# Where row weights, stores, exponentials and the last output groups stand in a convolution-attention-MoE kernel

## The chip, the cores and the metric

The kernel runs on one core of one Trainium2 chip. A core has a matrix engine (TensorE, called PE in the profile), three engines for elementwise work (VectorE or DVE, ScalarE or ACT, GpSimd or POOL), a synchronisation engine (SyncE or SP) that issues most transfers, and 16 DMA engines. The metric is the device time of one execution in microseconds (us); lower is better. "Before" is the median of 3 runs, 1987.64 us (1986.89 to 1988.37). One further execution was profiled.

## What is computed

The input x has two images of 256 channels and 56 x 56 pixels, in float32. Two layers follow.

Layer 0 works on each image: group norm, a 1x1 convolution to 768 channels (q, k and v), a depthwise 3x3 convolution of these, and 7 x 7 neighbourhood attention with 8 heads of 32 channels. The first four heads use dilation 1, the other four dilation 2. A projection is added to x.

```python
x = x + _L0_conv_ref(_gn(x), w_qkv1, w_qkv2, rpb0, rpb1, w_proj)
t = _to_tokens(x)                          # 2 * 3136 = 6272 tokens of 256
t = t + _L1_attn_ref(_ln_t(t), ...)        # linear attention and a feed-forward net
t = t + _L1_ffn_ref(_ln_t(t), ...)         # 8 experts, the best 2 for each token
```

Layer 1 works on the tokens. `_L1_attn_ref` is linear attention (elu + 1 on queries and keys) with a merge, two layer norms and a feed-forward net of width 512. `_L1_ffn_ref` routes each token to the two experts with the largest logits. The two weights follow from the difference of the two logits by one exponential. Each expert is a gelu net of 256 to 1024 to 256. The weighted sum of both experts is added to the token.

## The kernel before

All matmuls are in float32. The work is arranged so that PE always has something to do, and its own order is written out by hand (`tc.manual_schedule`). The order on the other engines comes from a scheduler at build time, which takes priorities, readiness and the ties `tc.issue_after(x)` ("not ahead of x") into account. What one engine does is therefore a fixed queue, and an instruction whose operand is late holds up all that stand behind it on that engine. The stages, in us from the span's start:

- 0 to 440: convolutions, and attention of image 1.
- 440 to 745: convolutions of image 2 together with the linear layer on the first half of the tokens (`linear(ph, tk, 0)`). Letters in `parts` say the order: keys, queries, message, feed-forward, route, prob and so on.
- 735 to 1045: attention of image 2. The last groups' routing (`ending`) and the first expert tiles run beside it.
- 1045 to 1440: the linear layer on the second half, with expert tiles interleaved.
- 1440 to 1970: the remaining expert tiles, in 39 slots. 34 are full tiles of 256 rows and 5 are half tiles of 128.
- 1970 to 1991: reading, turning and storing the last groups of the output.

Tokens are handled in groups of 4 blocks of 128. `route` (L2028) finds the two experts of each token (`top_two`) and the place of its row in its experts' lists. The sums over tokens are the matmuls L2083 and L2084 with the result `slot` (L2086). `weights` (L2018) takes the exponential of the difference of the logits on ACT (L2021). After it `store` (L1981) puts the tokens themselves into the result array y2 from ACT's queue (L1985), and POOL scatters the normalised rows into the experts' lists xs (helper at L168). ACT also computes gelu (hT, L1611), and gelu and the exponential need different tables, which ACT_TABLE_LOAD changes.

An expert tile goes through three steps. `fetch` (L1534) reads the expert's number, issues the loads of its rows xr (L1543) and its weights (L1547, L1551), and computes the rows' weights `eq` and row numbers `idi` on DVE (L1557 to L1561). `turn` (L1570) transposes the rows on PE (px, L1576), applies the norm's scale (xe, L1579), loads the bias b2 (L1584) and starts the result yt with it (L1589). `run` (L1591) does the first matmuls (ph, L1607), gelu, the second matmuls (py, L1625), the weighted addition (L1631) and the scatter that adds the rows to y2. In a full tile ph and py are 32 matmuls each.

When attention of image 2 begins, `prepare` (L796) loads rows of queries and keys (ld, L803), which PE turns (x, L766), and `settle` (L771) copies them to qT0 (L775), kT0 (L778), qT1 (L784) and kT1 (L791). `fetch` of the attention loads tables for the position bias (tab, L713), bands load their values (v0, L862; v1, L982), and each block has scores (s_ps, L651), an exponential (L655), the product with the table (p, L656) and the product with the values (po, L665). At this change the space of the first half's token tiles goes over to the attention.

In the last stage `between` is called once for each slot. From slot `first` (29) on, in nine slots, it starts the `read` (L2340) of one output group from y2. One slot later `write` turns it on PE (pto, L2352), copies it (L2358) and stores it (L2364). Behind the slots, each engine reads the number of surplus tiles (`more`, L2389), which a branch would run; here there are none. Then the last five groups are read all together, turned and stored.

Of the kernel before, what the change touches and what calls it, by code (L numbers as in the profile page):

```python
# [64 lines left out]
FILLS = (0, 2, 12, 18, 24, 27, 33)  # L65
ENDING = (4, 6, 13, 15, 20)
XW = C + 4


def shape_constants():  # L70
# [56 lines left out]
def hybrid_kernel(ctx: ExitStack, tc: tile.TileContext, a: dict, out: bass.AP):  # L127
# [46 lines left out]

    evac_n = [0]

    newest = [None, None, None]

    def evac(dst, src):

# [425 lines left out]
    class Attention:  # L606
# [116 lines left out]
        def run(self):  # L723
# [47 lines left out]
            def settle(g, k, pm):  # L771

                r0 = 4 * g
                if k == 0:
                    nc.scalar.mul(qT0[:, 2 * r0 : 2 * r0 + 8, :].rearrange("p r c -> p (r c)"), pm[:, :G], SCALE)  # L775
# [578 lines left out]
    class Experts:  # L1354
# [179 lines left out]
        def fetch(self, t, nh, pools):  # L1534

            run = self.tk.run
            full = nh == 2 and t < NTA
            tab, k = (self.tab_h, t) if nh == 1 else (self.tab_a, t) if full else (self.tab_b, t - NTA)
            x = SimpleNamespace(t=t, nh=nh, full=full)
            xr = x.xr = pools.xr()[:, :nh, :]  # L1540
            e = self.value(tab.tab[0:1, 0, k : k + 1], E - 1)
            r = self.value(tab.tab[0:1, 1, k : k + 1], E * RG + (NDUM - 1) * ST)
            ins = nc.sync.dma_start(xr, xs[bass.ds(r, nh * P), :].rearrange("(p j) c -> p j c", j=nh))  # L1543
            if full:
                apart(ins.ins, [f"xfull{run}"], [f"xlate{run}", f"fill{run}"])
            x.w1 = self.w.tile([P, 2, FF], F32, name="w1e")
            nc.sync.dma_start(  # L1547
                x.w1, a["L1_ffn_W1"][bass.ds(e, 1)].rearrange("one (ct p) f -> p (one ct) f", p=P)
            )
            x.w2 = self.w.tile([P, NJ, C], F32, name="w2e")  # L1550
            nc.sync.dma_start(  # L1551
                x.w2, a["L1_ffn_W2"][bass.ds(e, 1)].rearrange("one (j p) d -> p (one j) d", p=P)
            )
            x.e = e
            x.eq = self.small.tile([P, 2], F32, name="eq")
            eq = x.eq[:, :nh]
            nc.vector.tensor_scalar(eq, xr[:, :, C + 3], tab.etm[:, k : k + 1], None, ALU.is_equal)  # L1557
            x.idi = self.small.tile([P, 2], mybir.dt.int32, name="idi", bufs=4)
            nc.vector.tensor_copy(x.idi[:, :nh], xr[:, :, C])  # L1559
            nc.vector.tensor_tensor(eq, eq, xr[:, :, C + 2], ALU.mult)  # L1560
            nc.vector.tensor_tensor(eq, eq, xr[:, :, C + 1], ALU.add)  # L1561
# [6 lines left out]
            return x  # L1568

        def turn(self, x, pools):  # L1570

            nh = x.nh
            px = pools.px()
            for ct in range(2):
                for j in range(nh):
                    nc.tensor.transpose(px[:, ct, j, :], x.xr[:, j, ct * P : (ct + 1) * P], ident)  # L1576
            x.xe = pools.xe()[:, :, : nh * P]
            for ct in range(2):
                newest[0] = nc.vector.tensor_scalar(  # L1579
                    x.xe[:, ct, :], px[:, ct, :nh, :].rearrange("p j t -> p (j t)"),  # L1580
                    x.sv[:, ct : ct + 1], x.sv[:, 2 + ct : 3 + ct], ALU.mult, ALU.add,
                ).ins
            b2 = pools.b2e()
            nc.sync.dma_start(  # L1584
                b2, a["L1_ffn_b2"][bass.ds(x.e, 1)].rearrange("one d -> (one d)").partition_broadcast(P)
            )
            x.yt = pools.yt()
            for h in range(nh):
                nc.gpsimd.tensor_scalar(x.yt[:, h, :], b2, x.eq[:, h : h + 1], 1.0, ALU.mult, ALU.mult)  # L1589

        def run(self, ts, pools, between=lambda i: None):  # L1591
# [7 lines left out]
            for i, (t, nh) in enumerate(ts):  # L1599
# [4 lines left out]
                for j in range(NJ):  # L1604
                    p1 = pools.ph()[:, : nh * P]
                    for ct in range(2):
                        nc.tensor.matmul(  # L1607
                            p1, x.w1[:, ct, j * P : (j + 1) * P], x.xe[:, ct, :],
                            start=(ct == 0), stop=(ct == 1),
                        )  # L1610
                    nc.scalar.activation(hT[:, j, :], p1, AF.Gelu, bias=x.sv[:, 4 + j : 5 + j])  # L1611
                    if j % 2:
                        yield
                between(i)
# [32 lines left out]
    def linear(ph, tk, half, behind=None):  # L1647
# [290 lines left out]
        def feed_forward(n0, n, m2T, out):  # L1938
# [3 lines left out]
            for oc in range(4):  # L1942
                p1 = ps_h.tile([P, 512], F32, name="p1", tag="h")
                for k in range(4):
# [1 line left out]
                    nc.tensor.matmul(  # L1946
                        p1[:, :w], fw1[:, k, oc * P : (oc + 1) * P], rhs, start=(k == 0), stop=(k == 3)
                    )
                nc.scalar.activation(hT[:, oc, :w], p1[:, :w], AF.Relu, bias=hb[:, oc : oc + 1])
                yield  # L1950
            ss = sm.tile([P, 4], F32, name="ssf")
            lb = routing[-1].sm.tile([P, 4, E], F32, name="lb")
# [28 lines left out]
        def store(n0, n):  # L1981

            for k0 in range(0, n, 2):
                kn = min(2, n - k0)
                ins = nc.scalar.dma_start(  # L1985
                    y2[(n0 + k0) * P : (n0 + k0 + kn) * P, :].rearrange("(n p) c -> p n c", p=P),
                    tk.at(n0 + k0, kn),
                )
# [29 lines left out]
        def weights(rt, ms, row, n):  # L2018

            r = rt.sm.tile([P, 4], F32, name="rsum")[:, :n]  # L2020
            nc.scalar.activation(ms[1], ms[1], AF.Exp)  # L2021
# [154 lines left out]
    def layer1(whole, tk, conv_ctx=None, conv=None, behind=None):  # L2176


        run = tk.run
        conv = conv or none  # L2180

        def fill(n=1):
            for _ in range(n):
# [64 lines left out]
        def experts():  # L2248
# [5 lines left out]
        xc = experts() if run else None  # L2254
        pools = SimpleNamespace(
            turn=lambda: tc.issue_after(newest[1]),
            xr=lambda: xc.tile([P, 2, XW], F32, name="xr"),
            xe=lambda: xc.tile([P, 2, ST], F32, name="xe"),
            yt=lambda: xc.tile([P, 2, C], F32, name="yt"),
# [24 lines left out]

        with ExitStack() as ph:
            ln = linear(ph, tk, 1)
            pools.px = lambda: ln.ps_a.tile([P, 2, 2, P], F32, name="px", tag="a")
            pools.ph = lambda: ln.ps_q.tile([P, 2, ST], F32, name="ph", tag="q")[:, 0, :]
            summed = []
# [25 lines left out]
        with ExitStack() as ph:  # L2315
# [8 lines left out]
            ps_t = ph.enter_context(tc.tile_pool(name="p4pt", bufs=2, space=PSUM, reuse_waits="tile"))  # L2324
            pools = SimpleNamespace(
                turn=nullcontext,
                xr=lambda: xp.tile([P, 2, XW], F32, name="xr"),
                xe=lambda: xp.tile([P, 2, ST], F32, name="xe"),
                yt=lambda: xp.tile([P, 2, C], F32, name="yt"),
# [17 lines left out]
            def write(n0, n, yr, engines, places):  # L2347
                for ct in range(2):
# [12 lines left out]
                    for b in range(B):  # L2361
                        c0, c1 = max(n0 * P, b * T), min((n0 + n) * P, (b + 1) * T)
                        if c0 < c1:
                            engines[ct].dma_start(  # L2364
                                ov[b, ct, :, c0 - b * T : c1 - b * T], o_sb[:, c0 - n0 * P : c1 - n0 * P]
                            )

# [6 lines left out]

            def between(i):

                if held:
                    write(*held.pop(0), (nc.scalar, nc.scalar), [(ps_t, "pt")] * 2)
                if first <= i < first + early2:
                    held.append(read(*order[i - first], True))  # L2380
# [8 lines left out]
            more = nc.values_load(  # L2389
                ex.more[0:1, 0:1], min_val=0, max_val=NTL,  # L2390
                skip_runtime_bounds_check_because="the number of tiles is bounded by the counts",
            )
            with tc.If(more > 0):
                for _ in ex.run([(t, 2) for t in range(NFS, NTL)] + [(k, 1) for k in range(NHS, E)], pools):
                    pass
            last = [read(n0, n, False) for n0, n in order[early2:]]
            for h in held + last:
                write(*h, (nc.scalar, nc.sync), [(ps_t, "pt"), (ps_h, "ph")])

    with ExitStack() as ph:  # L2400
# [3 lines left out]
        rest = first_image(conv, ph)  # L2404
        layer1(ph, tokens, conv_ctx, rest, anchors["residual4"])
    bad = nc.values_load(
        bad[0:1, 0:1], min_val=0, max_val=1, skip_runtime_bounds_check_because="a comparison's result"
    )
    with tc.If(bad > 0):
        with ExitStack() as ph:  # L2410
# [39 lines left out]
```

## Time and profile before

| | us |
|---|---|
| median of 3 runs | 1987.64 |
| the profiled execution's own time | 1992.68 |
| its span, first to last instruction | 1990.9 |
| busy: PE, DVE, ACT, POOL | 1840.8, 1092.3, 705.9, 584.9 |
| last stage: one full tile, ph and py | 6.9 + 6.9 |
| from the end of the last py to the end of the span | 23.5 |

The profiled execution is 5.0 us longer than the median, so sums on the profile are made against 1992.68. Its mean granted TensorE clock was 0.97 of full speed. In the answers of the profile a line holds, for a wait, the waiting engine with tile and line, who released it, and then the total in us, the number of waits and the longest; on a timeline it holds the start in us, the length, the engine, the line, the operation with output <- input and sizes, the number of instructions drawn together, and in brackets how long the engine had been idle and who released it. "SPq" and "ACTq" are transfers issued from these engines.

### The profile page before, as it was taken

The numbers are of one execution on the slowest core, as the hardware profiler recorded it, in microseconds if no ns is written. First come the engines' busy times: TensorE is split into PE (matmuls) and PEld (weight loads), VectorE is DVE, ScalarE is ACT, GpSimd is POOL, SyncE is SP. The second block draws the span as 40 slices with busy tenths as digits, with TensorE's granted clock in tenths as the row PEclk, the third lists the DMA queues.
The fourth block names the chain that finished last, engine by engine and source line by source line (L and its number), as shares of the span: only waits on it lengthen the run. The fifth ranks groups of instructions, "written<-read, shape, count | busy, mean of one in ns | idle before, by whom it ended". The sixth has DMA issues, their size and how long they took to land.

```text
span 1990.9 us, 27720 instructions
## 1 busy us (share of the span) xinstructions
PE 1840.8 (92%) x9996; PEld 1306.9 (66%) x9996; DVE 1092.3 (55%) x2727; ACT 705.9 (35%) x1337; POOL 584.9 (29%) x634
## 2 busy tenths in 40 slices
PE   6999899988899997999989989999899999999996
PEld 3544454556555654666668756577788888888885
DVE  6887988889897646465547334555532212121221
ACT  2333324334433323545536443323322222323332
POOL 4630132025102344111126311445422222222221
PEclk9999899999999995999999999999999999999998
DMA  4753422350014235664474110115477676767995
GB/s 113 158 131 114 141 86 80 93 167 17 25 43 111 84 86 179 161 160 125 130 199 130 56 35 32 50 59 150 147 227 201 190 199 190 199 190 196 297 282 164
DMA packets 200152, 268.85 MB, mean 135 GB/s; under 512 B 30952, under 2 KB 158614, under 8 KB 199760
## 3 DMA queue, kind: packets, MB, share of 16 engines
q1 hardware_dynamic: 167920, 223.95, 37.6%
q0 software_dynamic: 19728, 27.54, 7.5%
q10 hardware_dynamic: 12352, 15.43, 2.3%
q8 instruction: 83, 1.36, 0.3%
q14 instruction: 69, 0.57, 0.1%
HBM read 200.19 MB, written 70.95 MB: 136 GB/s over the span
## 4 chain that ended last, share of the span: by engine, by line
PE 49%; DMA 4%; DVE 3%; ACT 3%; issue 1%; POOL 1%; SPq 0%; ACTq 0%; DVEq 0%; POOLq 0%
PE py L1625 13%; PE ph L1607 13%; PE p L1946 4%; PE x L1625 2%; PE x L1607 2%; DMA y<-yt,idi 2%; PE py L1962 2%; PE po L665 2%; DMA xr<-xs 1%; PE pm L1916 1%; PE kx L316 1%; PE x L358 1%; PE kp L304 1%; PE s_ps L651 1%; PE pq L1876 1%; PE px L1576 1%
## 5 line engine op out<-in xcount | busy, mean ns | idle before, releaser
L1607 PE MATMUL ph<-xe,w1e 128*128 128x256 f32 (+1 forms) x1448 | 311.3, 371 | 12.8 <-ACT hT L1611 7.9
L1625 PE MATMUL py<-w2e,hT 128*128 128x256 f32 x1392 | 311.4, 380 | 0.0
L1611 ACT ACTIVATE hT<-ph,sv 128x256 f32<-128x256 f32 (+1 forms) x362 | 165.6, 462 | 390.1 <-PE ph L1607 377.3
L1607 PEld LDWEIGHTS ph<-xe,w1e 128*128 128x128 f32 x1448 | 262.7, 191 | 52.0 <-ACT hT L1611 10.1
L1625 PEld LDWEIGHTS py<-w2e,hT 128*128 128x128 f32 x1392 | 260.3, 190 | 33.0 <-issue 0.2
L168 POOL DMA_INDIRECT y<-yt,idi x101 | 160.2, 1587 | 326.7 <-DVE yt L1631 188.7
L578 DVE SCALAR_TENSOR_TENSOR yc<-ypad,w,yc 128x1120 f32<-128x1120 f32 x144 | 202.5, 1410 | 28.4 <-ACT yc L568 26.0
L262 POOL TENSOR_TENSOR rs<-rs,mhalf 128x2 f32<-128x2 f32 (+3 forms) x90 | 72.8, 812 | 324.1 <-DVE rs L261 276.0
L528 PE MATMUL py<-x_sb,wq 128*128 128x448 f32 (+1 forms) x384 | 154.2, 533 | 7.2 <-ACT ypad L534 5.6
L655 ACT ACTIVATE p<-s_ps 112x952 f32<-112x952 f32 (+5 forms) x88 | 102.1, 1160 | 150.6 <-PE s_ps L651 101.4
L1559 DVE CAST idi<-xr 128x2 int32<-128x2 f32 (+1 forms) x53 | 10.1, 191 | 255.1 <-DMA xr<-xs 255.1
L656 DVE TENSOR_TENSOR p<-p,tab 112x952 f32<-112x952 f32 (+5 forms) x88 | 122.0, 1389 | 48.6 <-ACT p L655 41.3
L549 PE MATMUL pc<-ypad,diag 128*128 128x448 f32 x324 | 131.4, 547 | 0.0
L1631 DVE SCALAR_TENSOR_TENSOR yt<-py,eq,yt 128x256 f32<-128x256 f32 x87 | 41.8, 482 | 156.6 <-PE py L1625 156.5
L1589 POOL TENSOR_SCALAR yt<-b2e,eq 128x256 f32<-128x256 f32 x101 | 52.2, 522 | 253.5 <-DMA b2e<-in_L_ffn_b 214.9
L168 POOL DMA_INDIRECT xs<-row,si x98 | 97.5, 995 | 70.2 <-DVE si L2092 40.2
L528 PEld LDWEIGHTS py<-x_sb,wq 128*128 128x128 f32 x384 | 71.7, 197 | 69.4 <-issue 55.5
L571 DVE SCALAR_TENSOR_TENSOR yc<-ypad,w,yc 128x784 f32<-128x784 f32 x96 | 104.9, 1113 | 1.3 <-ACT yc L568 0.9
L665 PE MATMUL po<-p,v 98*32 98x170 f32 (+5 forms) x960 | 71.1, 378 | 30.3 <-DVE p L656 15.5
L549 PEld LDWEIGHTS pc<-ypad,diag 128*128 128x128 f32 x324 | 60.0, 191 | 52.3 <-issue 48.5
L1946 PE MATMUL p<-m2T,fw 128*128 128x512 f32 (+2 forms) x224 | 93.8, 542 | 0.0
L1946 PE MATMUL p<-xT,fw 128*128 128x512 f32 (+1 forms) x208 | 92.7, 568 | 0.0
(392 smaller groups left out, 2889.0 us busy)
## 6 DMA issues: line engine op xcount, KB each, us to landing
w1e<-in_L_ffn_W SPq DMA_DIRECT2D x53, 1024.0 KB
w2e<-in_L_ffn_W SPq DMA_DIRECT2D x53, 1024.0 KB
yd<-yc SPq DMA_DIRECT2D x24, 784.0 KB
ld<-yd SPq DMA_DIRECT2D x28, 448.0 KB
xr<-xs SPq DMA_DIRECT2D x48, 260.0 KB
b2e<-in_L_ffn_b SPq DMA_DIRECT2D x53, 128.0 KB
t<-td SPq DMA_DIRECT2D x12, 512.0 KB
y<-t ACTq DMA_DIRECT2D x24, 256.0 KB
```

The source lines that it names most:

```text
L168: ins = nc.gpsimd.indirect_dma_start(out=dst[:, :], out_offset=bass.IndirectOffsetOnAxis(ap=index, axis=0), in_=src, in_offset=None, **kw,)
L528: nc.tensor.matmul(py[:, :n, :], self.wq1[:, ct, oc * P : (oc + 1) * P], self.x_sb[:, ct, (q0 + g0) * WW : (q0 + g0 + n) * WW], start=(ct ...
L549: nc.tensor.matmul(pc, diag[:, tap, :], ypad[:, dy : dy + SHARE, dx : dx + WW], start=(tap == 0), stop=(tap == 8),)
L571: nc.vector.scalar_tensor_tensor(yc[:, y0:y1, :], src, w, yc[:, y0:y1, :], ALU.mult, ALU.add)
L578: nc.vector.scalar_tensor_tensor(yc[:, y0:y1, :], src, w, yc[:, y0:y1, :], ALU.mult, ALU.add)
L655: nc.scalar.activation(p[:nk, :, :n], s_ps[:nk, :, :n], AF.Exp)
L656: nc.vector.tensor_tensor(grid(p), grid(p), table[:nk], ALU.mult)
L665: nc.tensor.matmul(dst[hs] if w is None else den[hs], v[:nk, hs] if w is None else w[:nk, :], p[:, h, :, o : o + q.shape[2]], start=first ...
L1607: nc.tensor.matmul(p1, x.w1[:, ct, j * P : (j + 1) * P], x.xe[:, ct, :], start=(ct == 0), stop=(ct == 1),)
L1611: nc.scalar.activation(hT[:, j, :], p1, AF.Gelu, bias=x.sv[:, 4 + j : 5 + j])
L1625: nc.tensor.matmul(py, hT[:, j, h * P : (h + 1) * P], x.w2[:, j, :], start=(j == 0), stop=(j == NJ - 1),)
L1946: nc.tensor.matmul(p1[:, :w], fw1[:, k, oc * P : (oc + 1) * P], rhs, start=(k == 0), stop=(k == 3))
```

## The change

It has four parts.

1. The row weights leave `fetch` for a function `weigh` of their own. Tiles that run beside attention (`pools.beside`, only in the first pass, `run == 0`) call it in `turn`, after xe; all others call it in `fetch` where it stood.
2. The exponential of `weights` and the stores of `store` are tied behind the newest of the activations qT0, hT and hTl (`newest[3]`), which three places now set. The scheduler may not place them ahead of it.
3. In the first pass the number of surplus tiles is no longer read and branched on. DVE adds it to the flag `bad`, which in the end decides on a general path that computes everything again.
4. With `HELD = 3` the last three of the nine groups written between slots are kept until after the last tile. The reads of the first two of the five remaining groups are issued ahead of them, the other three behind. Their copies are shared between ACT and DVE, all of their six stores are issued from ACT, and they use PSUM of two pools.

```diff
+HELD = 3
-    newest = [None, None, None]
+    newest = [None, None, None, None]
...
                 if k == 0:
-                    nc.scalar.mul(qT0[...], pm[:, :G], SCALE)
+                    newest[3] = nc.scalar.mul(qT0[...], pm[:, :G], SCALE).ins
...
-            x.eq = self.small.tile([P, 2], F32, name="eq")
...
+            x.etm, x.eq = tab.etm[:, k : k + 1], None
+            if not pools.beside:
+                self.weigh(x)
...
+        def weigh(self, x):
+            xr, nh = x.xr, x.nh
             x.eq = self.small.tile([P, 2], F32, name="eq")
             eq = x.eq[:, :nh]
+            nc.vector.tensor_scalar(eq, xr[:, :, C + 3], x.etm, None, ALU.is_equal)
             x.idi = self.small.tile([P, 2], mybir.dt.int32, name="idi", bufs=4)
             nc.vector.tensor_copy(x.idi[:, :nh], xr[:, :, C])
             nc.vector.tensor_tensor(eq, eq, xr[:, :, C + 2], ALU.mult)
             nc.vector.tensor_tensor(eq, eq, xr[:, :, C + 1], ALU.add)
...
         def turn(self, x, pools):
...
+            if x.eq is None:
+                self.weigh(x)
             b2 = pools.b2e()
...
-                    nc.scalar.activation(hT[:, j, :], p1, AF.Gelu, bias=x.sv[:, 4 + j : 5 + j])
+                    newest[3] = nc.scalar.activation(
+                        hT[:, j, :], p1, AF.Gelu, bias=x.sv[:, 4 + j : 5 + j]
+                    ).ins
...
-                nc.scalar.activation(hT[:, oc, :w], p1[:, :w], AF.Relu, bias=hb[:, oc : oc + 1])
+                newest[3] = nc.scalar.activation(hT[:, oc, :w], p1[:, :w], AF.Relu, bias=hb[:, oc : oc + 1]).ins
...
         def store(n0, n):
...
-                ins = nc.scalar.dma_start(
+                with tc.issue_after(newest[3]):
+                    ins = nc.scalar.dma_start(
...
         def weights(rt, ms, row, n):
...
-            nc.scalar.activation(ms[1], ms[1], AF.Exp)
+            with tc.issue_after(newest[3]):
+                nc.scalar.activation(ms[1], ms[1], AF.Exp)
...
+            beside=run == 0,
...
-                if held:
+                if held and i <= first + early2 - HELD * (run == 0):
                     write(*held.pop(0), (nc.scalar, nc.scalar), [(ps_t, "pt")] * 2)
...
+            rest = order[early2:]
+            last = []
+            if run == 0:
+                nc.vector.tensor_tensor(bad, bad, ex.more[0:1, 0:1], ALU.max)
+                last += [read(n0, n, False) for n0, n in rest[:2]]
+                for h in held:
+                    write(*h, (nc.scalar, nc.vector), [(ps_t, "pt"), (ps_h, "ph")])
+                held.clear()
+            else:
...
-            last = [read(n0, n, False) for n0, n in order[early2:]]
+            last += [read(n0, n, False) for n0, n in rest[len(last) :]]
             for h in held + last:
                 write(*h, (nc.scalar, nc.sync), [(ps_t, "pt"), (ps_h, "ph")])
```

More of the change, by code (lines that the diff above doesn't have):

```diff
@@ L774, in settle @@
                 if k == 0:
-                    nc.scalar.mul(qT0[:, 2 * r0 : 2 * r0 + 8, :].rearrange("p r c -> p (r c)"), pm[:, :G], SCALE)
+                    newest[3] = nc.scalar.mul(
+                        qT0[:, 2 * r0 : 2 * r0 + 8, :].rearrange("p r c -> p (r c)"), pm[:, :G], SCALE
+                    ).ins
                 elif k == 2:
@@ L1554, in fetch @@
             x.e = e
-            x.eq = self.small.tile([P, 2], F32, name="eq")
[L1556 to L1561, printed above, removed]
+            x.etm, x.eq = tab.etm[:, k : k + 1], None
+            if not pools.beside:
+                self.weigh(x)
             so = self.small.tile([P, 4 + NJ, E], F32, name="so")
@@ L1568, in fetch @@
             return x
+        def weigh(self, x):
+            xr, nh = x.xr, x.nh
+            x.eq = self.small.tile([P, 2], F32, name="eq")
+            eq = x.eq[:, :nh]
+            nc.vector.tensor_scalar(eq, xr[:, :, C + 3], x.etm, None, ALU.is_equal)
+            x.idi = self.small.tile([P, 2], mybir.dt.int32, name="idi", bufs=4)
+            nc.vector.tensor_copy(x.idi[:, :nh], xr[:, :, C])
+            nc.vector.tensor_tensor(eq, eq, xr[:, :, C + 2], ALU.mult)
+            nc.vector.tensor_tensor(eq, eq, xr[:, :, C + 1], ALU.add)
         def turn(self, x, pools):
@@ L1610, in run @@
                         )
-                    nc.scalar.activation(hT[:, j, :], p1, AF.Gelu, bias=x.sv[:, 4 + j : 5 + j])
+                    newest[3] = nc.scalar.activation(
+                        hT[:, j, :], p1, AF.Gelu, bias=x.sv[:, 4 + j : 5 + j]
+                    ).ins
                     if j % 2:
@@ L1984, in store @@
                 kn = min(2, n - k0)
-                ins = nc.scalar.dma_start(
-                    y2[(n0 + k0) * P : (n0 + k0 + kn) * P, :].rearrange("(n p) c -> p n c", p=P),
-                    tk.at(n0 + k0, kn),
-                )
+                with tc.issue_after(newest[3]):
+                    ins = nc.scalar.dma_start(
+                        y2[(n0 + k0) * P : (n0 + k0 + kn) * P, :].rearrange("(n p) c -> p n c", p=P),
+                        tk.at(n0 + k0, kn),
+                    )
                 if (n0, n) in order[early1:]:
@@ L2180, in layer1 @@
         conv = conv or none
+        newest[3] = None
         def fill(n=1):
@@ L2286, in layer1 @@
             ln = linear(ph, tk, 1)
+            pools.beside = False
             pools.px = lambda: ln.ps_a.tile([P, 2, 2, P], F32, name="px", tag="a")
@@ L2326, in layer1 @@
                 turn=nullcontext,
+                beside=False,
                 xr=lambda: xp.tile([P, 2, XW], F32, name="xr"),
@@ L2363, in write @@
                         if c0 < c1:
-                            engines[ct].dma_start(
+                            (nc.sync if engines[ct] is nc.sync else nc.scalar).dma_start(
                                 ov[b, ct, :, c0 - b * T : c1 - b * T], o_sb[:, c0 - n0 * P : c1 - n0 * P]
@@ L2388, in layer1 @@
                         chunk(work)
[L2389 to L2395, printed above, removed]
-            last = [read(n0, n, False) for n0, n in order[early2:]]
+            rest = order[early2:]
[7 more added lines that the diff above has]
+            else:
+                more = nc.values_load(
+                    ex.more[0:1, 0:1], min_val=0, max_val=NTL,
+                    skip_runtime_bounds_check_because="the number of tiles is bounded by the counts",
+                )
+                with tc.If(more > 0):
+                    for _ in ex.run([(t, 2) for t in range(NFS, NTL)] + [(k, 1) for k in range(NHS, E)], pools):
+                        pass
+            last += [read(n0, n, False) for n0, n in rest[len(last) :]]
             for h in held + last:
@@ L2406, in hybrid_kernel @@
     bad = nc.values_load(
-        bad[0:1, 0:1], min_val=0, max_val=1, skip_runtime_bounds_check_because="a comparison's result"
+        bad[0:1, 0:1], min_val=0, max_val=NTL,
+        skip_runtime_bounds_check_because="a comparison's result or a number of tiles",
     )
```

## The prediction

> **What bounds the kernel now.** I read the page first, then TensorE's (PE's) waits, then the timelines around the longest of them.
>
> ```profile
> PE 1840.8 (92%) x9996; PEld 1306.9 (66%) x9996; DVE 1092.3 (55%) x2727; ACT 705.9 (35%) x1337; POOL 584.9 (29%) x634
> PEclk9999899999999995999999999999999999999998
> ```
>
> PE is busy for 92% of the span, and saturated from about 1440 us to the last matmul. A shift of PE before 1440 therefore reaches the end whole. The clock row has one dark slice, the sixteenth (747 to 796 us): the turn from the linear layer to the second image's attention. PE's waits, with total, number and longest in us:
>
> ```profile
> PE po L665 <- DVE p L656: 15.5, 11, 6.8
> PE pto L2352 <- DMA yr<-y: 10.9, 1, 10.9
> PE ph L1607 <- ACT hT L1611: 7.9, 5, 5.8
> PE x L766 <- ACT qT L775: 3.8, 1, 3.8
> ```
>
> The change touches all four. The 5.8 us one, on the timeline of all engines:
>
> ```profile
> 1389.90 1.28 ACT L2021 ACT_TABLE_LOAD   x1
> ...
> 1395.57 0.15 DVE L2080 TENSOR_TENSOR m<-m,m 128x2 f32<-128x2 f32 x1
> ...
> 1395.76 0.20 ACT L2021 ACTIVATE m<-m 128x2 f32<-128x2 f32 x1 [4.58 <-DVE m L2080]
> ...
> 1395.98 1.28 ACT L1611 ACT_TABLE_LOAD   x1
> ...
> 1397.28 0.47 ACT L1611 ACTIVATE hT<-ph,sv 128x256 f32<-128x256 f32 x1
> ...
> 1397.80 1.65 PE L1607 MATMUL ph<-xe,w1e 128*128 128x256 f32 x3 [5.81 <-ACT hT L1611]
> ```
>
> The routing exponential (L2021) stands in ScalarE's (ACT's) queue before its operand is ready. Behind it wait the gelus hT, and PE waits for them. PE's and SyncE's (SP's) timelines at the turn:
>
> ```profile
> 747.99 1.76 PE L766 MATMUL x<-ident,ld 112*128 112x112 f32 x8 [3.76 <-ACT qT L775]
> ...
> 756.69 1.76 PE L766 MATMUL x<-ident,ld 112*128 112x112 f32 x8
> ...
> 785.12 1.16 PE L665 MATMUL po<-p,v 112*32 112x280 f32 x8 [6.78 <-DVE p L656]
> ```
>
> ```profile
> 664.36 0.89 SPq L803 DMA_DIRECT2D ld<-yd  x2
> 674.62 78.70 SPq L713 DMA_DIRECT2D tab<-fp  x15
> 762.41 0.84 SPq L803 DMA_DIRECT2D ld<-yd  x2
> 763.34 2.15 SPq L862 DMA_DIRECT2D v<-yd  x3
> ```
>
> Before, the attention's first ld and tab loads were issued 70 to 90 us ahead of need, and the v loads after them. The tail, on PE and on SP:
>
> ```profile
> 1962.88 1.04 PE L2352 MATMUL pto<-ident,yr 128*128 128x128 f32 x8
> 1963.75 3.62 PE L1625 MATMUL py<-w2e,hT 128*128 128x256 f32 x16
> 1978.25 5.16 PE L2352 MATMUL pto<-ident,yr 128*128 128x128 f32 x26 [10.88 <-DMA yr<-y]
> ```
>
> ```profile
> 1973.21 2.37 SPq L2340 DMA_DIRECT2D yr<-y  x4
> ```
>
> After the last py (ends 1967.37) PE waits 10.88 us for scatter and reads, then transposes 26 blocks at half clock.
>
> **What the Trainium skill says.** "ScalarE: Activation LUTs", What ACT_TABLE_LOAD costs: about 1.28 us for a load, plus a drain. The trace has 1.28 us; it shows no drain of its own (exp begins 1395.76, load follows at 1395.98). "TensorE: Matmul & The Clock Gate", What's actually happening: an idle window of about 3.4 us halves the clock. The trace agrees: after the idle time at 1392 the clock record is 0.5 from 1395.53 to 1402.36. "DMA: Bandwidth & Descriptors", Issuing engines are not separate DMA queues: queues share the 16 engines. So stores put into the tail meet the scatter and the reads there; no run shows yet how much that costs.
>
> **Part 1, row weights at the turn.** Four DVE operations per tile change place for the tiles beside attention. In the order of the built kernels the first eq still stands between the same two DVE operations. Its 5.72 us wait for xr and PE's 6.78 us wait at 785.12 stay. Cost 0. A gain is bounded by 6.8 us, a loss by nothing shown; the unchanged order excludes both, so I take 0.
>
> **Part 2, stores and exponentials tied behind activations.** The number of table loads does not change (58 in both orders).
>
> *At 1390.* In the new order the exp comes after three more hT and two hTl. By then m (1395.57 on the old clock) is ready. PE's 5.81 us goes, and the next matmuls run at full clock: two groups of p L1946 took 1.06 us each after the stall and 0.61 a little later, so matmuls to 1402 lose some 2.3 us. Against that, pp (L2083) now meets its operand from DVE, ready at 1397 in both kernels, about 1 us early; and the gelu table load, moved to just before a tile's first hT (1413), is uncovered: 1.28 less the 0.3 us of slack, 1 us. A shorter wait at 1421.1 returns 0.8. Sum: -5.8 - 2.3 + 1.0 + 1.0 - 0.8 = -6.9; I take **-6.3**, since DVE's chain behind the late m also holds PE. From -7.5 to -4.
>
> *At the turn.* Exp after qT gains the 3.76 us wait only in part, since PE's next matmuls wait for DVE's `before` sum at 749.35 in both kernels. Then come three new delays.
> (a) x at 750.56 takes, in the new allocation, the PSUM buffer that DVE's slot (L2086) frees; that ends at 752.33 before, here about 752.6 by DVE's longer queue: PE is 1.9 us late.
> (b) The two y2 stores of the group (L1985; before at 720.5 and 723.9) now issue after the second qT and after qT1, about 754.1 and 755.8. The trace shows such a store landing 1.8 us after its 0.37 us issue: 758.0. The copy kT0 (L778, before 749.04) overwrites the stored tile's space and waits for it; 0.53 us later PE's x and s_ps go on, 3.4 us late.
> (c) SP has 16 v loads ahead of ld, and the first waits for ACT's sq (742.84 + 0.38 and its accumulator read, 743.4). At 0.72 us each (763.34: 2.15 us for 3), and with one waiting for a store's semaphore until 756.2, the ld loads issue at 757.7 and 758.2. In the trace ld loads land 4.3 and 5.2 us after issue: 762.4 and 763.8. PE wanted them at 756.69 and 757.11: now 6.5 late. The 15 tab loads at 0.8 us follow to 774.4, then the next ld, which lands at 779.0, 7.3 after 771.58.
> The last group's routing shifts with PE, and with it scatters, xr and eq at 782.97. Queued behind eq on DVE is p, for which po at 785.12 waits. Some 0.7 us are absorbed by 830. Sum +6.4. If PE keeps full clock from 747 to 774, since no idle stretch now fills a window, some 1.6 us come back. I take **+5.2**; +3.3 with the loads also early, +7.9 with them 1.5 us later.
>
> *Elsewhere* the exps of the linear groups moved while PE ran on: 0, hidden by PE's own matmuls; uncovered, 1 us each.
>
> **Part 3, surplus tiles left to the general path.** One register load per engine (0.27 to 0.68 us, 1945 to 1968) and a skipped branch go; one small DVE maximum comes. All lie beside the 1968 to 1973 wait for the scatter. 0.
>
> **Part 4, three output groups last.** Three writes leave PE's queue between expert tiles. Each cost the distance from pto's start to the next expert matmul: 1938.71 to 1939.99, 1950.85 to 1952.12, 1962.88 to 1963.75: 1.28 + 1.27 + 0.87 = 3.42 us. Their 24 transposes (3 us) now fill the 10.88 us wait. Their six stores bring 1.5 MB; at the reads' rate (1.66 MB in 4.9 us, 340 KB per us) 4.5 us of DMA beside the scatter and the reads, of which I let 0.6 reach the reads. The read of group 24 is now behind an ACT copy: 0.4. **-2.4**; from -4.4 (PE stays at full clock) to +0.6 (much of the 4.5 us lands on the reads).
>
> **Sum.** -6.3 + 5.2 - 2.4 = -3.5 us against the profiled execution of 1992.68 (span 1990.9, 1.8 around it): 1989.2. It stands 5.04 above the median 1987.64, so in the median **1984.1**. From no change the measurement tells 0.2%, 4.0 us: the case reaches both sides of 1983.7.
>
> **Rivals.**
> *Cheap turn.* The clock stays up, the ld loads land 1.5 us earlier: +2.5 rather than +5.2, and a tail of -4: 1987.6 - 6.3 + 2.5 - 4 = 1979.8. For it: fewer v loads in flight than at 763. Against: delay (b) needs nothing uncertain.
> *The stall only moves.* DVE's m waited 4.71 us for POOL's rs behind five scatters; PE's pp would wait for the same chain, and only 2.5 of 6.3 are gained: 1987.9. Against: PE has two groups of matmuls to run before pp.
> *Slower, through SP's queue at the turn.* 33 loads go through eight semaphores, each waiting for the load eight places ahead. Eight issues take 6 us; v loads landed 4.3 to 5.5 us after issue. If they take longer than 6, each of four laps adds the excess. At 8.5 the laps add 7.5 us and the sum is +4, from which it counts as slower; I put the case at 1994. For it: transfers of 56 KB in short rows, sharing with stores and scatters. Against: the measured 5.5.
> *Part 1 does act*: eq leaves DVE's queue and 785.12 is shortened; the order is against it, and it counts with the cheap turn.
>
> **Chances.** Main case 0.52, half on each side of 1983.7; cheap turn 0.19 (faster); stall moves 0.13 (same); slower 0.16. Faster 0.26 + 0.19 = 0.45; same 0.26 + 0.13 = 0.39; slower 0.16. The main case alone is 1980 to 1988; the range adds the cheap turn down to 1978.5 and the nearer part of the slower case, to 1992.
>
> **What would show it.** Right: no exp before hT at 1390 and PE's longest wait for hT below 1.5 us; on SP a row of v loads from 743 to 757 and ld only after; kT0's copy waiting for a DMA; PE's po near 785 starting about 7 us later; no pto between the last expert tiles. Wrong: tab or v loads landing late and PE waiting for them, a wait of several us for `chosen` at pp, or the reads of y landing more than 6 us after their issue.

## The result, and the profile after

The changed kernel takes 1992.8 us in the median of 12 runs, beside 1987.11 us for 12 runs of the kernel before. The ratio is 1.0035, with a 95% interval of 1.0020 to 1.0049: slower by 0.35%, some 7 us. The forecast was 3.5 us faster. The profiled execution took 1995.0 us (span 1992.8), that of before 1992.68 (span 1990.9).

The page of the changed kernel, busy times of the engines and PE's granted clock:

```profile
PE 1839.5 (92%) x9996; PEld 1303.9 (65%) x9996; DVE 1096.6 (55%) x2731; ACT 705.3 (35%) x1334; POOL 587.4 (29%) x634
PEclk9999999999999995999999989999899999999998
```

The totals say nothing: the same matmuls, nearly the same busy time. The dark slice of the turn is still the sixteenth; the 29th (1395 to 1445 us), 0.9 or more before, now has 0.8, and so has the 24th (1146 to 1196 us). PE's waits of the changed kernel tell more (total, number and longest, in us):

```profile
PE pto L2372 <- DMA yr<-y: 10.1, 1, 10.1
PE x L767 <- DMA ld<-yd: 9.8, 4, 5.8
PE po L666 <- DVE p L657: 8.6, 9, 1.3
...
PE pp L2099 <- DVE chosen L2090: 5.0, 2, 3.5
...
PE x L767 <- ACT kT L781: 2.4, 1, 2.4
```

The wait of 5.81 us for hT and the one of 3.8 us for qT0 are gone, and so is the longest one for p (6.8 before, 1.3 now). In their place stand 9.8 us for ld, 2.4 us for kT0, some 2 us each for kT1 and for DVE's slot, and 5.0 us for `chosen`.

**The turn.** SP's timeline after, and two stretches of PE's:

```profile
740.68 2.75 SPq L865 DMA_DIRECT2D v<-yd  x4
743.48 6.23 SPq L985 DMA_DIRECT2D v<-yd  x8
749.75 5.70 SPq L865 DMA_DIRECT2D v<-yd  x4
755.55 1.00 SPq L806 DMA_DIRECT2D ld<-yd  x2
756.63 21.95 SPq L714 DMA_DIRECT2D tab<-fp  x15
778.67 0.96 SPq L806 DMA_DIRECT2D ld<-yd  x2
```

```profile
757.22 1.01 PE L767 MATMUL x<-ident,ld 112*128 112x112 f32 x4 [2.40 <-ACT kT L781]
...
760.76 0.61 PE L767 MATMUL x<-ident,ld 112*128 112x112 f32 x2 [1.63 <-DMA ld<-yd]
763.01 1.38 PE L767 MATMUL x<-ident,ld 112*128 112x112 f32 x6 [1.64 <-DMA ld<-yd]
...
783.72 0.63 PE L767 MATMUL x<-ident,ld 112*128 112x112 f32 x2 [5.79 <-DMA ld<-yd]
```

And ACT's, where kT0 waits for a store:

```profile
752.39 0.37 ACTq L2000 DMA_DIRECT2D y<-t  x1
...
756.63 0.97 ACT L781 COPY kT<-x 128x448 f32<-128x448 f32 x2 [3.64 <-DMA y<-t]
```

The forecast order is all there, and PE's po of 785.12 starts 7.8 us later. Sixteen v loads stand ahead of ld. The ld loads issue at 755.55 and 756.07, and 15 tab loads hold the next pair until 778.67. By the completions recorded in the trace (here and below counted from the end of the issuing instruction) the first two ld loads took 4.6 and 6.4 us, where 4.3 and 5.2 had been assumed. The store at 752.39, for which kT0 waits, took 3.9 us, where 1.8 had been assumed.

The 15 tab loads take 21.95 us to issue rather than some 16. Each issue takes some 0.8 us; for the rest SP waits. Its waits from 740 to 800 say for what, and ACT's timeline shows the stores:

```profile
SPq L714 <- DMA y<-t: 6.2, 2, 5.5
SPq L714 <- DMA ld<-yd: 2.1, 2, 1.5
```

```profile
763.69 0.94 ACTq L2000 DMA_DIRECT2D y<-t  x2
```

These are two more tied stores, those of the group after. They land at 770.98 and 772.48, and the tab loads that wait for them issue at 771.00 and 772.54. In the kernel before, this pair was issued at 742.12 and 746.64, and each took 1.8 us.

**The second half.** From here times are those of the changed kernel's own trace. PE at 1390 to 1440:

```profile
1398.17 0.37 PE L2099 MATMUL pp<-chosen,tri 128*128 128x16 f32 x2 [1.49 <-DVE chosen L2090]
...
1411.03 1.99 PE L1619 MATMUL ph<-xe,w1e 128*128 128x256 f32 x8 [1.04 <-ACT hT L1623]
...
1429.07 0.37 PE L2099 MATMUL pp<-chosen,tri 128*128 128x16 f32 x2 [3.51 <-DVE chosen L2090]
...
1432.30 5.36 PE L1619 MATMUL ph<-xe,w1e 128*128 128x256 f32 x14 [0.40 <-DVE xe L1589]
```

Counted against before from 1380 on, PE is 8.6 us ahead when it comes to the first pp. There it loses 3.3 us: it waits 1.49 us for `chosen`, and the granted clock is 0.5 from 1398.9 to 1402.4. It loses 1.2 us around the uncovered gelu table load and gets 1.0 back at 1417. Then it loses 3.5 us at the second pp, and the granted clock is 0.5 from 1429.7 to 1436.5: 14 matmuls of ph take 5.36 us at 1432.30, while 12 of them took 2.86 us at full clock in the kernel before. By 1440 nothing is left of the gain. What the second pp waits for is on DVE's timeline:

```profile
1420.91 0.16 DVE L2070 TENSOR_TENSOR rs<-rs,rs 128x1 f32<-128x1 f32 x1 [0.66 <-POOL rs L2069]
1425.22 0.41 DVE L156 TENSOR_SCALAR row<-t_ab,mv,rs 128x256 f32<-128x256 f32 x1 [4.15 <-DMA xs<-row,si]
...
1428.75 0.17 DVE L2090 TENSOR_TENSOR chosen<-oh,oh 128x16 f32<-128x16 f32 x1
```

DVE has all the operands of the last group's normalised row at 1421. It may not write it, since the scatter of the group before (L169, xs<-row) still reads the same buffer: it waits 4.15 us. The routing (L2013 to L2028) and `chosen` stand behind it. POOL, ACT and SP just before, in this order:

```profile
1418.02 1.00 POOL L169 DMA_INDIRECT xs<-row,si  x1 [0.30 <-issue]
```

```profile
1416.57 0.37 ACTq L2000 DMA_DIRECT2D y<-t  x1
...
1418.30 0.45 ACTq L2000 DMA_DIRECT2D y<-t  x1
1418.84 1.41 ACTq L2000 DMA_DIRECT2D y<-t_ab  x1
```

```profile
1418.29 0.38 SPq L1550 DMA_DIRECT2D w1e<-in_L_ffn_W  x1
```

The scatter completes 6.0 us after its issue. Around it are the three tied stores (256, 256 and 128 KB) and the load of an expert's first weights (w1e, 1 MB). In the kernel before, the same scatter was issued at 1421.42. Of the three stores only the 128 KB one was near, issued at 1420.18 and complete at 1421.90; the load of w1e came at 1422.26. The scatter completed 2.4 us after its issue. The same row hardly waited:

```profile
1425.03 0.41 DVE L155 TENSOR_SCALAR row<-t_ab,mv,rs 128x256 f32<-128x256 f32 x1 [0.55 <-DMA xs<-row,si]
```

So the row stands at 1425 in both kernels, although POOL had come to the scatter 3.4 us earlier.

**The tail.** PE and SP after:

```profile
1962.67 3.62 PE L1639 MATMUL py<-w2e,hT 128*128 128x256 f32 x16
1966.12 2.78 PE L2372 MATMUL pto<-ident,yr 128*128 128x128 f32 x24
1978.98 4.82 PE L2372 MATMUL pto<-ident,yr 128*128 128x128 f32 x26 [10.08 <-DMA yr<-y]
```

```profile
1972.12 2.46 SPq L2360 DMA_DIRECT2D yr<-y  x4
1981.68 5.78 SPq L2384 DMA_DIRECT2D out<-o_sb  x6
```

The 24 transposes now stand in the wait, and no pto is left between the last tiles. From the start of the last py to that of the last 26 transposes it was 14.50 us before, and is 16.31 now. By the recorded completions the last scatter takes 3.41 us rather than 2.21, and the four reads of y from SP 6.4 to 7.2 us rather than 4.5 to 5.6. The last six stores of SP issue over 5.78 us.

Set against before, matmul by matmul, these are the stretches of PE's queue (us, a minus sign for a gain; the last column against a second profile of the kernel before, taken beside a third set of runs of the changed one, below):

| stretch, on the clock of before | forecast | first profiles | second pair |
|---|---|---|---|
| up to 740 | 0 | -2.7 | +3.2 |
| turn, 740 to 836 | +5.2 | +3.1 | +5.2 |
| 836 to 1380 | 0 | +0.8 | +0.9 |
| 1380 to 1440 | -6.3 | +0.3 | -2.0 |
| last stage up to 1938, from 1440 | 0 | +1.0 | +1.9 |
| from 1938 to the end | -2.4 | -0.6 | -2.5 |
| sum | -3.5 | +1.9 | +6.6 |

What differs up to 740 is there by 430 us, ahead of every instruction that the change moves, and its sign is not the same in the two pairs.

### The profile page after: what moved, and what is told of

Read it like the earlier page. It is cut to its first block, busy times and chain, and to the rows that moved or that the text cites. A ratio compares the mean times of both kernels' runs of the same rounds, so it can differ in the third digit from the quotient of the medians.

```text
span 1992.8 us, 27675 instructions
## 1 busy us (share of the span) xinstructions
PE 1839.5 (92%) x9996; PEld 1303.9 (65%) x9996; DVE 1096.6 (55%) x2731; ACT 705.3 (35%) x1334; POOL 587.4 (29%) x634
## 4 chain that ended last, share of the span: by engine, by line
PE 70%; DVE 14%; DMA 6%; ACT 4%; issue 2%; POOL 2%; SPq 1%; ACTq 0%; POOLq 0%; DVEq 0%
PE ph L1619 14%; PE py L1639 14%; PE p L1960 7%; PE po L666 4%; PE py L529 4%; PE py L1976 4%; PE pc L550 3%; DVE yc L579 3%; PE x L1639 2%; DVE yc L572 2%; PE s_ps L652 2%; PE x L1619 2%; PE pm L1930 2%; PE kp L305 1%; DMA xr<-xs 1%
## 5 line engine op out<-in xcount | busy, mean ns | idle before, releaser
L169 POOL DMA_INDIRECT y<-yt,idi x101 | 160.2, 1587 | 322.9 <-DVE yt L1645 182.9
L169 POOL DMA_INDIRECT xs<-row,si x98 | 97.6, 996 | 82.0 <-DVE row L2042 33.3
L1976 PE MATMUL py<-fw,hTl 128*128 128x264 f32 x392 | 89.8, 386 | 0.0
```

The source lines that it names most:

```text
L169: ins = nc.gpsimd.indirect_dma_start(out=dst[:, :], out_offset=bass.IndirectOffsetOnAxis(ap=index, axis=0), in_=src, in_offset=None, **kw,)
L1976: nc.tensor.matmul(py[:, : C + E], hT[:, kk, c0 : c0 + P], fw2[:, kk, :], start=(kk == 0), stop=(kk == 3),)
```

## The experiments

Three sets were run, each beside its own runs of the kernel before, and each kernel in five rounds. Ratios are to the kernel before of the same set, with 95% intervals.

My theory after the first comparison: the tied stores of the second half cost the gain at 1390, through the scatter and the reused row; those of the first half cost the turn; the exponentials alone keep their gain. The rival: exponentials moved to later are themselves the reason for the late `chosen`, whatever the stores do ("the stall only moves").

### First set: each tie alone (before: 1997.55 us, 38 runs)

*Exponentials alone*: `newest[3]` is set in the three places as in the change, and only the exponential is tied.

```diff
-            nc.scalar.activation(ms[1], ms[1], AF.Exp)
+            with tc.issue_after(newest[3]):
+                nc.scalar.activation(ms[1], ms[1], AF.Exp)
```

> The kernel before with only the exponential of the routing weights tied behind the newest activation; stores, row weights and last groups as before. In its built order SP's queue at the turn is that of before, and at 1390 us the exponential stands behind three more hT. Theory A (the moved stores gave back the gain, by delaying the scatter that row2 waits for at 1421): PE's 5.8 us wait at 1397 is gone, pp near 1425 waits less than 1 us for chosen, and the time is 4 to 7 us below before. Theory B (the stall only moves on, with or without stores): pp (L2083) waits 3 us or more for chosen once or twice before 1440, and the time is within 2 us of before.

Measured: 1988.29 us, ratio 0.9953 [0.9935, 0.9971]: some 9 us below before, more than the 4 to 7 expected. PE gains 5.9 us from 1380 to 1440 and loses 0.5 of it up to the end. Its longest wait there is for hT, and there is none for `chosen`:

```profile
PE ph L1609 <- ACT hT L1613: 3.4, 3, 1.6
```

*Stores alone*: the same three places, and only `store` is tied.

```diff
+                with tc.issue_after(newest[3]):
-                ins = nc.scalar.dma_start(
+                    ins = nc.scalar.dma_start(
```

> The kernel before with only the y2 stores tied behind the newest activation. In its built order 16 v loads stand ahead of ld on SP, as in the changed kernel. Theory A (the stores make the turn slow): PE at 830 to 840 us is 3 to 7 us late against before, x waits for ld loads 8 us or more in all, the 5.8 us wait for hT at 1390 stays, and the time is 4 to 8 us above before. Theory C (the turn's loss comes from the exponentials' new places): within 2 us of before.

Measured: 1996.16 us, 0.9996 [0.9982, 1.0009]. The stores' tie moves the exponential at 1390 too, since the scheduler fills ACT's queue anew: the stall goes, which theory A did not expect, and PE is 7.6 us ahead of its 1380 place at 1400. By 1440 it is 0.8 us behind it. The turn is 4.6 us longer than in the first profile of before, and yet the time is within 2 us of before, as theory C had it (more on this under "What stays open"). PE's and DVE's waits of this kernel from there:

```profile
PE pp L2088 <- DVE chosen L2079: 4.3, 1, 4.3
```

```profile
DVE row L155 <- DMA xs<-row,si: 3.8, 1, 3.8
```

The gain and its loss thus both occur without the change's tie on exponentials.

*Parts 3 and 4 alone*: `HELD`, the three late writes, and the surplus tiles left to the general path.

```diff
...
-                if held:
+                if held and i <= first + early2 - HELD * (run == 0):
...
```

> The kernel before with only the surplus tiles left to the general path and three groups kept to the end. Theory D (the held stores delay scatter and reads): last py ends 3.4 us earlier, but the stretch from there to the span's end grows from 23.5 to about 26.5 us, and the time is within 1.5 us of before. Theory E (the tail's loss in the changed kernel was chance): that stretch stays below 24.5 us and the time is 2 to 3 us below before.

Measured: 1996.78 us, 1.0001 [0.9985, 1.0016]. PE gains 3.5 us up to the last py, as computed, and the end gives 1.7 back: from the last py to the end of the span it takes 25.2 us, between what the two theories expected. What remains, some 1.8 us, lies inside the interval.

*All but the stores*: the change with `store` as before.

```diff
-                with tc.issue_after(newest[3]):
-                    ins = nc.scalar.dma_start(
+                ins = nc.scalar.dma_start(
```

> The changed kernel with the stores untied, all else as changed. Theory A: 5 to 8 us below the changed kernel, so 0 to 3 us below before if the exponentials gain nothing, and 4 to 7 below before if they do. Theory C: as slow as the changed kernel, 5 to 7 us above before.

Measured: 1989.87 us, 0.9955 [0.9939, 0.9970]: no different from the exponentials alone. Parts 1, 3 and 4 together are worth nothing that these runs tell, and the stores are what separates the change from a faster kernel.

### Second set: which stores, and by what (before: 1999.79 us, 44 runs)

*The changed kernel again*:

> The changed kernel itself, on the chip and in the call of the next three. Against before 0 to 0.5% slower again (it was 0.35%). PE waits 3 us or more for chosen near 1429, as in its first profile.

Measured: 1996.9 us, 0.9986 [0.9973, 0.9999]. In this set the changed kernel is not slower. The verdict of the first measurement did not repeat, and that called for the third set. Inside the set the comparisons still hold.

*Stores tied in the first half only*:

```diff
-                with tc.issue_after(newest[3]):
+                with tc.issue_after(newest[3]) if (n0, n) in order[:early1] else nullcontext():
```

> The changed kernel with the stores tied only for the groups of the first half (those before and at the turn), untied in the second half. Theory A1 (the turn makes it slow): as slow as the changed kernel, within 2 us, ld loads late as there. Theory A2 (the stores of the second half give the exponentials' gain back at 1421 to 1440): the wait for chosen near 1429 is below 1 us, PE reaches the last stage 5 to 7 us earlier than in the changed kernel, and the time is 5 to 7 us below it.

Measured: 1992.13 us, 0.9956 [0.9941, 0.9971], 4.8 us below the changed kernel of the same set.

*Stores tied in the second half only*:

```diff
-                with tc.issue_after(newest[3]):
+                with tc.issue_after(newest[3]) if (n0, n) in order[early1:] else nullcontext():
```

> The changed kernel with the stores tied only for the groups of the second half; at the turn SP's queue is that of before. Theory A1: 4 to 7 us below the changed kernel. Theory A2: within 2 us of the changed kernel, with the wait of 3 us or more for chosen near 1429.

Measured: 1993.17 us, 0.9970 [0.9960, 0.9980]. This is 3.7 us below the changed kernel, between what the two theories expected, and the two intervals overlap. The profiled execution took 1998.09 us, so its trace can't tell where the 3.7 us come from. The medians of the two halves are close, but the waits are where the theory puts them. PE's and DVE's waits around the second pp, first-half ties:

```profile
PE pp L2099 <- DVE chosen L2090: 0.5, 1, 0.5
```

```profile
DVE row L156 <- DMA xs<-row,si: 1.7, 1, 1.7
```

and second-half ties:

```profile
PE pp L2099 <- DVE chosen L2090: 3.7, 1, 3.7
```

```profile
DVE row L156 <- DMA xs<-row,si: 3.5, 1, 3.5
```

Over 1380 to 1440 PE gains 4.2 us with first-half ties and 1.1 with second-half ties (the changed kernel of this set loses 1.4). The scatter completes 3.6 us after its issue with the first, 5.4 with the second. Over all profiles it takes 1.9 to 2.4 us in the other seven whose second-half stores are free, and 5.4 to 6.7 in the six where they are tied.

*The last group's row in a buffer of its own*: everything as in the changed kernel, stores where they are, but the row of the one-block group comes from the pool of the four-block rows and so overwrites nothing that a scatter is still reading.

```diff
-            if n == 4:
-                row = lp.tile([P, 4, XW], F32, name="row")
+            if n != 2:
+                row = lp.tile([P, 4, XW], F32, name="row")[:, :n]
```

> The changed kernel, but the normalised rows of the last group (24, 1) go to a tile of the pool lp rather than to the space of group (45, 2), whose scatter must have landed. If the chain store, late scatter, row, chosen, pp is right: DVE's wait of 4.2 us for xs ahead of row<-t_ab is gone, pp waits less than 1 us for chosen near 1429, and the time is 4 to 6 us below the changed kernel. If the wait for chosen has another cause: it stays, and the time is within 2 us of the changed kernel.

Measured: 1991.14 us, 0.9956 [0.9937, 0.9976], 5.8 us below the changed kernel of the same set. The scatter is as slow as ever (5.5 us), but DVE no longer waits for it, and PE's wait is short:

```profile
PE pp L2099 <- DVE chosen L2090: 0.7, 1, 0.7
```

PE gains 5.5 us over 1380 to 1440, so nearly the whole forecast. This settles the place: the rewritten buffer is what turns a slow scatter into a late `chosen`. The late exponential is untouched here, so the rival falls. What slows the scatter is shown only as far as the tie. In all kernels with it the load of w1e also comes earlier against the scatter (between 1.0 us ahead of its start and 0.3 behind, 0.8 behind in the others), and no run has the stores without that load or the load without the stores.

### Third set: the turn, with a control (before: 1987.79 us, 57 runs)

In the first two sets the kernel before took 1998 and 2000 us, in the first measurement and in this set 1987 and 1988. The first and third sets ran on one chip, so the chip alone doesn't set this level.

*The kernel before as a control*, no edit:

> The kernel before once more, as a control: its ratio to the kernel before, with its interval, says what these comparisons can tell apart, 0.9985 to 1.0015. Its trace says how long the turn takes here without any change: PE from 740 to 836 us of the first profile took 96 us there, and 99 to 104 us in four kernels with an unchanged turn since. If that slower turn is a matter of chip or run, it is slower than 98 us here too; if it comes from those kernels' edits elsewhere, 95 to 97 us.

Measured: 1986.23 us, 0.9993 [0.9976, 1.0010]: two copies of one kernel differ by less than 0.2%, as assumed.

*The turn alone*: the kernel before with `store` tied in the first half only, and the exponentials free.

```diff
+                with tc.issue_after(newest[3]) if (n0, n) in order[:early1] else nullcontext():
-                ins = nc.scalar.dma_start(
+                    ins = nc.scalar.dma_start(
```

> The kernel before with only the stores of the first half tied, so that only the turn is built differently. Theory F (the turn costs what was predicted): PE from 740 to 836 takes 4 to 7 us more than in before_again, and the time is 4 to 7 us above before. Theory G (the turn's new waits stand where the old order loses about as much): within 2 us of before, although x waits for ld.

Measured: 1994.64 us, 1.0036 [1.0019, 1.0052]. PE's waits from 740 to 850 in this kernel, and then in the control:

```profile
PE x L766 <- DMA ld<-yd: 10.9, 4, 4.8
PE x L766 <- ACT qT L775: 4.4, 2, 3.8
...
PE x L766 <- ACT kT L780: 1.6, 1, 1.6
```

```profile
PE po L665 <- DVE p L656: 7.0, 2, 6.7
PE x L766 <- ACT qT L775: 3.8, 1, 3.8
```

From 740 to 836 the control gains 2.4 us on the first profile of before, and this kernel loses 3.0: the ties cost 5.4 us. Here the 3.8 us wait for qT0 stays, and yet the turn costs as much as in the changed kernel: to remove that wait gains nothing. From 1380 to 1440 the stall stands as in the control (a difference of 0.1 us).

*The changed kernel, third time*:

> The changed kernel in one call with the kernel before and the exponentials alone. It was 0.35% slower than before at first and 0.14% faster in a later call. If that is a matter of the chip, it is between -0.3% and +0.4% here; against the exponentials alone 5 to 8 us slower.

Measured: 1992.97 us, 1.0026 [1.0013, 1.0039]: slower again. The turn costs 5.2 us against the control. PE's waits from 1380 to 1440 in this kernel, then in the control:

```profile
PE pp L2099 <- DVE chosen L2090: 5.3, 2, 3.7
```

```profile
PE ph L1607 <- ACT hT L1611: 7.4, 3, 5.8
```

*Exponentials alone, again*:

> The exponentials alone tied, in one call with the changed kernel: 0.3 to 0.6% below before, and 5 to 8 us below the changed kernel. If its first result was a matter of the chip: within 0.2% of before.

Measured: 1979.93 us, 0.9960 [0.9945, 0.9974], 13.0 us below the changed kernel of the same set, where 5 to 8 were expected. PE gains 5.9 us from 1380 to 1440, or 6.8 against the control, and pp is not waited for. DVE's row waits hardly at all:

```profile
DVE row L155 <- DMA xs<-row,si: 0.2, 1, 0.2
```

This is the fastest version: below the kernel before in two sets, and below both kernels wherever it stood beside them.

**What stays open.** In the first two sets the turn of kernels whose first-half stores are free is 4.1 to 7.7 us longer than in the first profile of before, where the third set's is 2.4 to 2.5 shorter. The kernels with tied stores lose 4.6 to 6.5 there, so the ties cost next to nothing in those sets. This may account for the changed kernel's 0.9986 there beside 1.0026 and 1.0035 in the other two measurements; the cause of the longer turns is not known. In a turn with free stores of the first set, ACT's copy kT1 stands still with no releaser that the profile can name:

```profile
767.31 0.25 ACT L184 COPY kT<-x 128x112 f32<-128x112 f32 x1 [3.76 <-remote]
```

The semaphore for which it waits is one of PE's. Its update is recorded at 767.28, while the matmuls of PE ahead of it are shown to end at 762.57. What held it was not found, and no run was aimed at it. Open, too, is a part of the size. In the second pair the stretches that the change touches (turn, 1380 to 1440, the end) sum to +0.7, and another 2.8 arises between them, in the stages of 836 to 1380 and 1440 to 1938, where two profiles of one kernel differ by 1 us; the medians say 4 to 10.

## Why the prediction was right or wrong

The forecast time was wrong: 1984.1, with a range to 1992.0. By the ratio on the median of the prediction the changed kernel stands at 1994.6. The likeliest sign was wrong too, while the terms for the turn and for parts 1 and 3 were of the right size.

**At 1390: the step that failed.** The term was -6.3. Its own part is right: the exponentials alone give -5.9, or -6.8 against the control. The failure is in the sentence that costs the moves of the second tie elsewhere at nothing. It speaks of the linear groups' exponentials and says nothing of the second half's stores, which the new order puts at 1416.57 to 1418.84, around a scatter. The sum also ended with "a shorter wait at 1421.1 returns 0.8" and did not ask what is late next. DVE's row at 1425 was already waiting for a scatter before (0.55 us), so a PE that comes 7 us earlier had no slack there. The first pp was priced at 1.0 us; its wait is 1.49, and the half clock behind it, which only the first of three profiles of the changed kernel has, cost 1.7 more. The second pp, which had no price, cost 3.5 us and some 2 more by the half clock. In place of -6.3 the stretch gives +0.3, -2.0 (against the control) and +1.4 in three profiles of the changed kernel, and the two runs that undo the cause from both ends (stores freed, buffer separated) gain 4.2 and 5.5 us where the changed kernel beside them loses 1.4.

**The gelu load at 1413** was priced at 1 us uncovered: 1.04 measured at 1411.03.

**The turn.** +5.2 was forecast, and +5.2 and +5.4 were measured against the control; +3.1 against the first profile of before, whose own turn was 2.4 us longer than the control's. The size is right, but two errors in it cancel: at 785 PE had lost 10.5 us against the control (6.4 + 0.7 forecast), and 5 of them were absorbed by 836 (0.7 forecast). The three delays exist. (a) The wait for DVE's slot is 2.1 us (1.9 forecast). (b) PE waits 2.4 us for kT0 (3.4 forecast). (c) The waits for ld come to 9.8 us. The second load of the first pair took 1.2 us longer than assumed, and the tabs 6 us longer to issue, most of which the later wait for p took up (6.78 us before, 1.3 at most now). These 6 us are the wait for the stores issued at 763.69: the prediction followed one pair of stores to the turn and left out the next. Its 774.4 for the end of the tabs is also more than its own numbers give, as 15 loads at 0.8 us are 12 and not 16. The hope that the clock would stay up was vain: it was 0.5 from 747.0 to 791.4.

**The tail.** -2.4 was forecast; -0.6 and -2.5 came out, and about -1.8 for this part alone. The 3.42 us before the last py are confirmed (3.5). The 0.6 us allowed for the stores' share in the transfers was too small: scatter +1.2 us and reads +1.4 to +1.8 us in the first profile. The page "DMA: Bandwidth & Descriptors" of the Trainium skill (Issuing engines are not separate DMA queues), from which the prediction took that stores would meet scatter and reads, agrees with the slower scatter and reads here, and with the scatter of 6.0 us rather than 2.4 at 1418, where it was not applied.

**Parts 1 and 3** were put at 0; with them and part 4 or without all three (all but the stores, exponentials alone) the ratios are 0.9955 and 0.9953.

**The rivals.** "The stall only moves" named the place, pp waiting for `chosen`, but neither the whole size of the loss nor the cause: POOL's rs was ready at 1420.9, and it was the scatter that was late. Its price let 2.5 of the 6.3 be gained; with the whole 6.3 lost, the prediction's own sum would have been +2.8, slower than before by less than 0.2%, and this was not priced as a case. "Slower, through SP's queue" did not decide: SP's tab loads did wait for earlier loads, but for 3.0 us in all (2.1 for ld, 0.9 for a tab), and by 836 the turn stood at the main case's value. Its sum was off too: four laps of 2.5 us are 10, not 7.5. "Cheap turn" did not happen in the third set.

**What would show it.** All the signs named for "right" appeared, and three of those named for "wrong" too: PE waiting for late loads (ld, 5.8 us), several us at pp for `chosen`, and reads of y landing more than 6 us after issue (6.4 to 7.2; 4.5 to 5.6 before).

## What to carry to other kernels

When an edit pulls one engine forward, follow the chain past the wait that goes, to the next instruction with little slack, and count a small wait there (0.55 us here) as the sign that the gain ends there. A store moved in an engine's queue has two prices, the issue and the delay of what is beside it: a scatter that took 6.0 us rather than 2.4, a row of loads that stood 6.2 us until two stores had landed. It matters where a buffer is rewritten that the other transfer still reads. A tie made for one reason (exponentials) should not be handed to a second kind of instruction (stores) without asking the same of it.

## What the runs showed of the hardware

- The same indirect scatter of 128 rows completed 1.9 to 2.4 us after its issue in seven profiles where one 128 KB store stood just ahead of it and a 1 MB load 0.8 us behind its start, 3.6 us after it in an eighth, and 5.4 to 6.7 us after it in the six where 640 KB of stores and the 1 MB load were issued between 2.7 us ahead and 0.9 us behind.
- At the turn, the second of the first two ld loads completed 4.8 to 5.2 us after its issue in the seven profiles with free first-half stores, and 6.2 to 9.5 us after it in the seven where 16 loads of v stand directly ahead.
- The last two y2 stores of the first half completed 1.8 us after their issue at 742 and 747 us in the kernel before, and 6.9 and 7.9 us after it at 764 in the changed kernel, with the ld and tab loads in flight.
- After a wait of 3.51 us on PE the granted clock was 0.5 from 1429.7 to 1436.5, although matmuls ran from 1429.07 on; 14 matmuls of ph in it took 5.36 us. By the 2.86 us for 12 matmuls at full clock, that stretch alone lost 2 us. A stretch of half clock goes with this wait in all five profiles where it is 3.5 us or longer; with the 1.5 us wait at the first pp one goes in only two of six.
- The same program had a level of 1987 to 1988 us in the first measurement and the third set, and of 1998 to 2000 us in the first and second sets, the first on the chip of the third. Differences of 0.3% hold only within a set, and even so the turn's share of them changed with the set.
